# Moving one fold, one adding up and the verdict in a graph attention and convolution kernel

## The chip, the cores and the metric

The kernel runs on one core of a Trainium2 chip. The metric is the device time of the whole program in microseconds, lower is better; the kernel before takes 2567.88 us as the median of three runs.

The engines are named as in the profile: PE is TensorE, PEld its weight loads, DVE is VectorE, ACT is ScalarE, POOL is GpSimd, SP is SyncE, which here issues most DMAs.

## What is computed

For each of 32 batches of a 512 x 512 block x, with one adjacency matrix adj for all:

```
q, k, v = x @ Wq + bq, x @ Wk + bk, x @ Wv + bv         # 8 heads of 64
w   = softmax(q k^T / sqrt(64) + (-1e9 where adj == 0))  # per head, over keys
x   = layernorm(x + w v)                                 # no gain or shift
y   = adj @ x
out = layernorm(x + y @ W1 + b1)
```

All inputs and outputs are float32.

## The kernel before, in words

**Precision.** A large product is made as three passes of split factors (HIGH, REST, BOTH), each of four matmuls of 128x512. HIGH and REST gather in a "near" PSUM bank, BOTH in a "far" one. The near bank is read first, the far one is added after it: for q and k by ACT (L435) and DVE (L436), for v by DVE twice (L466, L467). There are eight banks, taken in turn.

**Order.** Everything is unrolled in a region in which each engine issues its instructions in the order in which the Python code emits them (`manual_schedule`). The order across engines comes from semaphores. `merge(units, behind)` emits unit k and then the list `behind[k]`.

**A batch.** `iteration(b)` ends batch b's attention while it projects batch b + 1. Heads come in pairs hp = 0 to 3, and pairs in groups g of two:
- `scores` makes, for each pair and each block j of keys, two score blocks on PE (L609), masks them on DVE (L611), takes exponentials on ACT (L613) and adds the blocks j on POOL into a tile `es` (L624). There are two `es` buffers; so es(b, hp) overwrites es(b, hp - 2), and es(b + 1, 0) overwrites es(b, 2).
- `fold_squares(b, hp)` turns `es` around in squares of 32 (two DVE transposes, L662) and sums them (two reductions, L664). `pass_parts` and `fetch_parts` carry the partial sums through DRAM on SP's queue (L671, L678), and `add_up` finishes the denominators of a group: a reduction and a reciprocal on DVE (L684, L685), and a sum on POOL for a guard (L686).
- `attend(b, hp)` multiplies exponentials and values on PE (L632), with `V[b, j]` for block j, j = 0 to 3 in turn. `turn_out` turns the result on DVE (L644) and sends it through DRAM; `fetch_rows` brings it back in rows (L652), `scale_rows` scales by the denominators on ACT (L698), `add_rows` adds to x on POOL (L702).

**Around the first part of the change.** For b = 0 the code emits: projections of batch 1, units 0 to 3 (q and k of blocks 0 and 1), with folds and add_up between; attend and turn_out of pairs 2 and 3; scaling of rows; then

```
        later = scores(b + 1, 0)
        run(added + later + folded[1:])
```

`scores(b + 1, 0)` emits the POOL sums of pair 0 itself and returns those of pair 1 as `later`; `added` are the residual adds of POOL. Then come units 4 to 7 of the projections, with the passing of parts behind the first, fold (1, 0) behind the third; then the values of batch 1, with `add_up(0, 1)` behind row block 0 and fold (1, 1) and DMA issues (loads of the next x in squares L232, rows L652, weight chunks L419) behind row block 1. After the values, for b = 0, come DVE turns of batch 2's x (L347), `split_last_weight` (emitted before the last three turns: ACT L766, L767, L770 and POOL L768, L771), the splits of batch 2's x (ACT L304, DVE L307, POOL L310), and iteration 1 begins with attend (1, 0) and (1, 1), their turn-outs, and scores (1, 1).

**Around the second part.** The last batch's four row blocks r end the kernel one after the other: DVE adds the far bank (L568), takes statistics (L484, L485), ACT takes the root (L488), DVE inverts it (L493) and makes a shift (L495), ACT normalises (L500), SP stores (L515). The last row block is normalised in two halves, one by DVE (L1009), one by ACT (L1011), which are stored from SP and from ACT (L1013). The guards of the whole run are summed by a 1-column matmul (L991) and compared to one number, `verdict` (L1007). After that every engine loads the verdict (L168) and branches on it (L170), past a general kernel that isn't run when the guards hold.

Of the kernel before, what the change touches and what calls it, by code (L numbers as in the profile page):

```python
# [12 lines left out]
AF = mybir.ActivationFunctionType  # L13
ALU = mybir.AluOpType
# [4 lines left out]
P = 128  # L19
# [163 lines left out]
def fast_kernel(ctx: ExitStack, tc, verdict, x, adj, Wq, bq, Wk, bk, Wv, bv, W1, b1, out):  # L183
    nc = tc.nc
# [3 lines left out]
    NB = N // P  # L188
# [11 lines left out]
    def bank(*shape):  # L200

        return psum.tile([P, *shape], FP, name="bank", tag="bank", bufs=8)
# [159 lines left out]
    def turns(b):  # L362
        return [(turn_squares, b, d) for d in range(DB)] if b < B else []

    def splits_of_x(b):
        return [[(f, b, d) for d in range(DB)] if b < B else [] for f in (high_of_x, rest_of_x, both_of_x)]
# [102 lines left out]
    def projections(b):  # L469

        return [(project, b, which, m) for which, m in SEQUENCE] if b < B else []
# [4 lines left out]
    STAT, RSTD, SHIFT, HIGHS, LOWS = {}, {}, {}, {}, {}  # L476
# [13 lines left out]
    def invert_root(t, slots):  # L490

        rstd = RSTD[t][:, slots]
        nc.vector.reciprocal(rstd, rstd)  # L493
        for slot in range(slots.start, slots.stop):
            nc.vector.tensor_scalar(SHIFT[t][:, slot:slot + 1], STAT[t][:, slot, 0:1], RSTD[t][:, slot:slot + 1], -1.0,  # L495
                                    op0=ALU.mult, op1=ALU.mult)
# [95 lines left out]
    def aggregation(b):  # L592

        return [[(f, b, d) for d in range(DB)] if b >= 0 else [] for f in (split, aggregate)]
# [31 lines left out]
    def attend(b, hp):  # L626
        po = bank(N)
        for j in range(NB):
            e = E.pop((b, hp, j))
            for s in range(2):  # L630
                h = 2 * hp + s
                nc.tensor.matmul(po[s * HD:(s + 1) * HD, :], V[b, j][:, h * HD:(h + 1) * HD], e[:, s, :],  # L632
                                 start=(j == 0), stop=(j == NB - 1))
        OUT[b, hp] = po

    def turn_out(b, hp):

        po = OUT.pop((b, hp))
        at = AT[b, hp] = work.tile([P, N], FP, name="attT")
        if b == B - 1:  # L640
            nc.scalar.activation(at, po, AF.Copy)  # L641
            return

        nc.vector.transpose(at, po)  # L644
        TURNED[b, hp] = passing.tile([P, N], FP, name="turned")
        nc.sync.dma_start(TURNED[b, hp], at)
# [26 lines left out]
    def fetch_parts(b, g):  # L673

        part = PART[b, g].rearrange("p a c h -> p a (c h)")
        passed = PASSED.pop((b, g)).rearrange("(a r) i x -> i r a x", r=SQ)
        for i in range(P // SQ):
            nc.sync.dma_start(part[i * SQ:(i + 1) * SQ, :, :], passed[i])  # L678
# [49 lines left out]
    def run(units):  # L728
        for unit in units:
            unit[0](*unit[1:])  # L730
# [3 lines left out]
    pm = bank(P)  # L734
# [46 lines left out]
    def folds(b, g):  # L781
        return [(fold_squares, b, hp) for hp in range(g * PAIRS, (g + 1) * PAIRS)]
# [5 lines left out]
    def residuals(b, g):  # L788

        return [[(f, b, hp) for hp in range(g * PAIRS, (g + 1) * PAIRS)] for f in (scale_rows, add_rows)]  # L790
# [4 lines left out]
    def merge(units, behind):  # L795

        merged = []
        for k in range(max(len(units), len(behind))):
            merged += units[k:k + 1] + (behind[k] if k < len(behind) else [])
        return merged  # L800

    def take_scores(b, g):
        run(scores(b, g))

    def iteration(b):

        units = projections(b + 1)
        scaled, added = residuals(b, 0)
        later_scaled, later_added = residuals(b, 1)
        turned, divided = turns(b + 2), splits_of_x(b + 2)  # L810
        splits, gathered = aggregation(b - 1)
        squares = [(load_squares, b + 2, d) for d in range(DB)]
        folded = folds(b, 1)

        attend(b, 0)
        turn_out(b, 0)
        sooner, later = AFTER.pop(b - 1, ([], []))
        run(sooner)
        attend(b, 1)
        turn_out(b, 1)  # L820
        if b > 0:
            fetch_parts(b, 0)
        take_scores(b, 1)
        run(later)
        waiting = [(fetch_rows, b, 0), (fetch_rows, b, 1)]
        looking = 2 <= b < 2 + NB
        look = [(look_for_low_half, b - 2)] if looking else []
        ready = 1 if looking else 0 if b < 2 else 2
        run(waiting[:ready])
        if b == 0:  # L830
            run(merge(units[:4], [waiting + [(fold_squares, b, 1), (pass_parts, b, 0), (fetch_parts, b, 0)], [],
                                  [(add_up, b, 0)],
                                  folded[:1]]))
        else:
            old, young = norm(b - 1, 1), norm(b - 1, 0)
            roots = slice(0, 2 * NB if b > 1 else NB)
            if b == 1:
                run(survey(0, 0))
            run(merge(units[:4], [waiting[ready:]
                                  + [(square_root, b - 1, roots), (add_up, b, 0), (invert_root, b - 1, roots)],  # L840
                                  folded[:1] + old[2:], [(store, b - 2)] if b > 1 else [], young[2:] + scaled]))
        attend(b, 2)
        turn_out(b, 2)
        load(b)
        if looking:
            load_adjacency_rows(b - 2)
        attend(b, 3)
        turn_out(b, 3)
        if b == 0:
            run(scaled)  # L850
        later = scores(b + 1, 0)
        run(added + later + folded[1:])

        run(merge(units[4:], [[(pass_parts, b, 1), (fetch_parts, b, 1)], look, [(fold_squares, b + 1, 0)], splits[:2]]))
        units = values(b + 1)
        chunks = [(fetch_chunk, (b + 2) * len(SEQUENCE) + n) for n in range(AHEAD)]
        squares += [(fetch_rows, b, 2), (fetch_rows, b, 3), (pass_parts, b + 1, 0)] + chunks
        run(merge(units, [[(add_up, b, 1)], [(fold_squares, b + 1, 1)] + squares, later_scaled if b == B - 2 else [],
                          turned[:1] + (later_added if b == B - 2 else [])]))
        if b == B - 2:  # L860
            load(B - 1)
        if b == 0:
            split_last_weight()
        run(merge(gathered, [[unit] for unit in turned[1:]]))
        fresh, seen, shift = survey(b, 0), survey(b - 1), biases(b - 1)
        high, rest, both = divided
        if b == 0:
            run(high + rest + both[::-1] + later_scaled + later_added)
            return
        convolve(b - 1, FIRST_TWO)  # L870
        if b == B - 2:
            run([(add_row, b - 1, 0), (add_row, b - 1, 1)] + shift[:2] + fresh + seen[:2])
            return
        run(later_scaled + later_added[:1] + [(add_row, b - 1, 0)] + shift[:1] + later_added[1:])
        run([(add_row, b - 1, 1)] + shift[1:2] + seen[:1])
        convolve(b - 1, whole(2))
        run([(add_row, b - 1, 2)] + shift[2:3] + fresh[:1])
        convolve(b - 1, whole(3))
        run(high + rest + [(add_row, b - 1, 3)] + shift[3:] + both)
        AFTER[b] = (fresh[1:] + seen[1:2], seen[2:])  # L880
# [87 lines left out]
    for b in range(B - 1):  # L968
        iteration(b)
    last_halves(B - 1)  # L970

    t = B - 1
# [17 lines left out]
    pm = bank(N)  # L990
# [4 lines left out]
    for r in range(NB):  # L995
        slot = slice(NB + r, NB + r + 1)
        add_far(t, r, FAR.pop((t, r)))
        statistics(t, 1, r)
        square_root(t + 1, slot)
        if r < NB - 1:  # L1000
            add_near(t, r + 1, NEAR.pop((t, r + 1)))
        invert_root(t + 1, slot)
        if r < NB - 1:
            normalise(t + 1, NB + r)
            store(t, [r])
        if r == NB - 2:
            nc.vector.tensor_scalar(verdict, pm[0:1, 0:1], P - 0.5, None, op0=ALU.is_lt)  # L1007
    sides = [X[t][:, NB - 1, side * D // 2:(side + 1) * D // 2] for side in range(2)]
    nc.vector.tensor_scalar(sides[0], sides[0], STAT[t + 1][:, slot.start, 0:1], RSTD[t + 1][:, slot],  # L1009
                            op0=ALU.subtract, op1=ALU.mult)  # L1010
    nc.scalar.activation(sides[1], sides[1], AF.Identity, bias=SHIFT[t + 1][:, slot], scale=RSTD[t + 1][:, slot])  # L1011
    for side, engine in enumerate((nc.sync, nc.scalar)):
        engine.dma_start(out[t, (NB - 1) * P:, side * D // 2:(side + 1) * D // 2], sides[side])  # L1013


# [22 lines left out]
```

## Time and profile before

| What | Value |
|---|---|
| runs | 2567.47, 2567.88, 2568.14 us; median 2567.88 |
| the profiled execution | 2570.15 us; its span, first to last instruction, 2568.3 us |
| granted TensorE clock | 0.999 |
| PE busy | 2558.8 us, 100% |
| DVE, ACT, POOL busy | 2058.3, 1528.5, 1751.8 us |
| one sum of POOL, L624 | 2394 to 2407 ns |
| one masking of DVE, L611 | 678 ns |
| one exponential of ACT, L613 | 1055 ns |
| one score matmul, L609; one of attend, L632; one of a pass, L424 | 598; 595; 389 to 392 ns |

Times in the profile are microseconds from the first instruction. Durations overlap on an engine: sixteen L611 take 9.62 us, 0.598 from start to start. "Idle before, releaser" names what ended an idle stretch. PE's busy time counts a matmul that is held in the array by a full bank as busy, so a stretch is also to be compared with an equal one elsewhere.

### The profile page before, as it was taken

Reading aid. Unit: us, or ns where it says so; the run is one execution under the profiler, and the core shown is the slowest. Engines: PE = TensorE matmul, PEld = TensorE weight load, DVE = VectorE, ACT = ScalarE, POOL = GpSimd, SP = SyncE. Lnnn points to the kernel's source line nnn. Section 1 sums busy time; section 2 is a strip of 40 time slices with the busy share of each in tenths; the row PEclk is TensorE's granted clock in tenths of the full one; section 3 lists DMA queues with packets and bytes.
Section 4 is the critical chain, followed back from the end, with each engine's and each line's share of the span. In section 5 each row is a group of like instructions: output and inputs, shape, how many; then the busy total and the mean of one; then the engine's idle time right before and its main releaser. Section 6 shows DMA issues by size and latency. Waiting matters only on the chain.

```text
span 2568.3 us, 36882 instructions
## 1 busy us (share of the span) xinstructions
PE 2558.8 (100%) x11324; PEld 1692.3 (66%) x11324; DVE 2058.3 (80%) x3796; ACT 1528.5 (60%) x2540; POOL 1751.8 (68%) x1104
## 2 busy tenths in 40 slices
PE   9999999999999999999999999999999999999998
PEld 6676666666676666766667676666766667666666
DVE  8878878788787887877888778877787787887878
ACT  5656655666555666556665565655657556565555
POOL 4776667666676666766767676676766766666767
PEclk9999999999999999999999999999999999999999
DMA  9655554554545645456455465554655546555441
GB/s 266 167 158 150 161 154 117 165 156 151 166 113 150 168 138 163 125 138 177 136 156 133 133 174 138 164 133 123 173 143 160 148 113 167 146 158 163 108 121 52
DMA packets 747291, 380.59 MB, mean 148 GB/s; under 512 B 594896, under 2 KB 599248, under 8 KB 747088
## 3 DMA queue, kind: packets, MB, share of 16 engines
q1 hardware_dynamic: 746656, 377.51, 53.6%
q8 instruction: 93, 1.52, 0.3%
q14 instruction: 110, 0.90, 0.1%
q10 hardware_dynamic: 432, 0.66, 0.1%
HBM read 303.57 MB, written 74.45 MB: 147 GB/s over the span
## 4 chain that ended last, share of the span: by engine, by line
PE 99%; DVE 0%; DMA 0%; ACT 0%; issue 0%; DVEq 0%
PE bank L424 55%; PE bank L609 18%; PE bank L632 17%; PE bank L533 9%; PE bank L557 0%; DMA xin<-in_x_dram 0%; DVE bnst L484 0%; DVE xlast L564 0%; DVE xlast L568 0%; PE bank L336 0%; PE bank L708 0%; DVE shift L495 0%; PE bank L738 0%; ACT attT L641 0%; ACT xlast L1011 0%
## 5 line engine op out<-in xcount | busy, mean ns | idle before, releaser
L613 ACT ACTIVATE e<-e 128x1024 f32<-128x1024 f32 x512 | 525.7, 1055 | 309.0 <-DVE e L611 269.7
L424 PE MATMUL bank<-factors,stream 128*128 128x512 f32 x3012 | 703.2, 392 | 0.0
L424 PEld LDWEIGHTS bank<-factors,stream 128*128 128x128 f32 x3012 | 560.5, 188 | 163.4 <-DVE e L611 23.5
L624 POOL TENSOR_TENSOR es<-es,e 128x1024 f32<-128x1024 f32 x256 | 616.2, 2407 | 20.1
L611 DVE SCALAR_TENSOR_TENSOR e<-gap,bank 128x512 f32<-128x512 uint8 x1024 | 617.7, 678 | 12.5 <-PE bank L609 12.5
L624 POOL TENSOR_TENSOR es<-e 128x1024 f32<-128x1024 f32 x128 | 306.4, 2394 | 425.8 <-ACT e L613 423.4
L609 PE MATMUL bank<-q,k 64*128 64x512 f32 x2048 | 462.7, 598 | 0.0
L632 PE MATMUL bank<-e,v 128*64 128x512 f32 x2048 | 453.6, 595 | 0.0
L609 PEld LDWEIGHTS bank<-q,k 64*128 64x128 f32 x2048 | 203.2, 186 | 258.0 <-issue 159.0
L424 PE MATMUL bank<-w,factors 128*128 128x512 f32 x1536 | 354.3, 389 | 0.0
L424 PE MATMUL bank<-wv,factors 128*128 128x512 f32 x1536 | 353.5, 389 | 0.0
L698 ACT ACTIVATE rows<-rows,zero,inverse 128x64 f32<-128x64 f32 x992 | 335.1, 429 | 8.5 <-DVE inverse L685 8.5
L310 POOL TENSOR_TENSOR factors<-factors,factors 128x512 fp32r<-128x512 f32 x254 | 321.3, 1290 | 25.0 <-DVE factors L307 25.0
L424 PEld LDWEIGHTS bank<-wv,factors 128*128 128x128 f32 x1536 | 288.2, 188 | 60.6 <-DVE e L611 0.8
L424 PEld LDWEIGHTS bank<-w,factors 128*128 128x128 f32 x1536 | 288.0, 188 | 60.7 <-POOL factors L310 0.4
L632 PEld LDWEIGHTS bank<-e,v 128*64 128x64 f32 x2048 | 141.4, 137 | 278.4 <-issue 264.4
L510 ACT ACTIVATE high<-xs 128x512 fp32r<-128x512 f32 x124 | 74.4, 627 | 333.5 <-PE bank L533 333.4
L511 POOL TENSOR_TENSOR low<-xs,high 128x512 fp32r<-128x512 f32 x124 | 159.3, 1296 | 155.7 <-PE bank L533 155.7
L548 POOL TENSOR_TENSOR xs<-xs,b_r 128x512 f32<-128x512 f32 x124 | 160.3, 1294 | 125.7 <-DVE xs L568 125.7
L644 DVE STREAM_TRANSPOSE attT<-bank 128x512 f32<-128x512 f32 x124 | 87.8, 708 | 155.7 <-PE bank L632 152.8
L500 ACT ACTIVATE xs<-xs,shift,rstd 128x512 f32<-128x512 f32 x248 | 181.5, 805 | 14.8 <-DVE shift L495 14.8
L702 POOL TENSOR_TENSOR xs<-xs,rows 128x512 f32<-128x512 f32 x124 | 160.7, 1307 | 22.4 <-DMA stream<-kept_q 10.2
(98 smaller groups left out, 2431.4 us busy)
## 6 DMA issues: line engine op xcount, KB each, us to landing
stream<-kept_q SPq DMA_DIRECT2D x372, 256.0 KB, 4.7
stream<-kept_k SPq DMA_DIRECT2D x372, 256.0 KB, 3.6
xin<-in_x_dram SPq DMA_DIRECT2D x496, 64.0 KB, 2.3
turned<-attT SPq DMA_DIRECT2D x124, 256.0 KB, 3.3
rows<-turned SPq DMA_DIRECT2D x496, 64.0 KB, 2.5
xs<-in_x_dram SPq DMA_DIRECT2D x31, 1024.0 KB, 5.9
out_dram<-xs SPq DMA_DIRECT2D x31, 1024.0 KB, 5.2
part<-passed SPq DMA_DIRECT2D x256, 8.0 KB, 1.7
```

Source lines behind the costliest of these rows:

```text
L310: engine.tensor_sub(both, plain(high), plain(rest))
L424: nc.tensor.matmul(pm, left(f, d), right(f, d), start=(f != REST and d == 0), stop=(f != HIGH and d == DB - 1))
L500: nc.scalar.activation(row, row, AF.Identity, bias=SHIFT[t][:, slot:slot + 1], scale=RSTD[t][:, slot:slot + 1])
L533: nc.tensor.matmul(pm, part, adjT[:, n % NB, :], start=(n == 0), stop=(n == 2 * NB - 1))
L548: nc.gpsimd.tensor_add(X[b][:, c, :], X[b][:, c, :], b1_r)
L609: nc.tensor.matmul(ps[s], keys[:, j * P:(j + 1) * P], queries, start=True, stop=True)
L611: nc.vector.scalar_tensor_tensor(e[:, s, :], gap[:, j, :], NEG * root, ps[s], op0=ALU.mult, op1=ALU.add)
L613: nc.scalar.activation(e, e, AF.Exp, scale=1.0 / root)
L624: nc.gpsimd.tensor_add(ES[b, hp], ES[b, hp] if j > 1 else E[b, hp, 0], E[b, hp, j])
L632: nc.tensor.matmul(po[s * HD:(s + 1) * HD, :], V[b, j][:, h * HD:(h + 1) * HD], e[:, s, :], start=(j == 0), stop=(j == NB - 1))
L698: nc.scalar.activation(part, part, AF.Identity, bias=zero, scale=inverse[:, c, s:s + 1])
L702: nc.gpsimd.tensor_add(cols, cols, ROWS.pop((b, hp)))
```

## The change

For b = 0 alone, `fold_squares(0, 2)` moves from behind projection unit 3 to behind the scores of batch 1's first group, ahead of `fold_squares(0, 3)`, and `add_up(0, 0)` moves from behind unit 2 to behind unit 3. At the end of the kernel the verdict's comparison moves from ahead of the last row block's far sum to behind its root; the last row block's shift is no longer made, and both its halves are normalised by DVE, which subtracts the mean and multiplies by the inverted root.

```diff
         if b == 0:
-            run(merge(units[:4], [waiting + [(fold_squares, b, 1), (pass_parts, b, 0), (fetch_parts, b, 0)], [],
-                                  [(add_up, b, 0)],
-                                  folded[:1]]))
+            run(merge(units[:4], [waiting + [(fold_squares, b, 1), (pass_parts, b, 0), (fetch_parts, b, 0)], [], [],
+                                  [(add_up, b, 0)]]))
...
         later = scores(b + 1, 0)
-        run(added + later + folded[1:])
+        run(added + later + folded[b > 0:])
...
         square_root(t + 1, slot)
         if r < NB - 1:
             add_near(t, r + 1, NEAR.pop((t, r + 1)))
-        invert_root(t + 1, slot)
-        if r < NB - 1:
+            invert_root(t + 1, slot)
             normalise(t + 1, NB + r)
             store(t, [r])
-        if r == NB - 2:
-            nc.vector.tensor_scalar(verdict, pm[0:1, 0:1], P - 0.5, None, op0=ALU.is_lt)
+    nc.vector.tensor_scalar(verdict, pm[0:1, 0:1], P - 0.5, None, op0=ALU.is_lt)
+    rstd = RSTD[t + 1][:, slot]
+    nc.vector.reciprocal(rstd, rstd)
     sides = [X[t][:, NB - 1, side * D // 2:(side + 1) * D // 2] for side in range(2)]
-    nc.vector.tensor_scalar(sides[0], sides[0], STAT[t + 1][:, slot.start, 0:1], RSTD[t + 1][:, slot],
-                            op0=ALU.subtract, op1=ALU.mult)
-    nc.scalar.activation(sides[1], sides[1], AF.Identity, bias=SHIFT[t + 1][:, slot], scale=RSTD[t + 1][:, slot])
     for side, engine in enumerate((nc.sync, nc.scalar)):
+        nc.vector.tensor_scalar(sides[side], sides[side], STAT[t + 1][:, slot.start, 0:1], rstd,
+                                op0=ALU.subtract, op1=ALU.mult)
         engine.dma_start(out[t, (NB - 1) * P:, side * D // 2:(side + 1) * D // 2], sides[side])
```

## The prediction

> **What bounds the kernel now.** I first read the page's chain of waits and the waits of TensorE (PE).
>
> ```profile
> PE 99%; DVE 0%; DMA 0%; ACT 0%; issue 0%; DVEq 0%
> ```
>
> ```profile
> PE bank L738 <- DVE attT L733: 1.1, 1, 1.1
> ```
>
> The chain is PE nearly all the way, and PE's longest recorded wait is 1.1 us, at the start. So any microsecond PE loses or wins is carried to the end; work elsewhere costs nothing until PE waits for it. Next the timelines around batch 0's first pass: PE, then VectorE (DVE), then GpSimd (POOL). Columns are start, length, engine, line, operation, tiles.
>
> ```profile
> 82.00 8.21 PE L609 MATMUL bank<-q,k 64*128 64x512 f32 x32
> 90.14 11.20 PE L424 MATMUL bank<-factors,stream 128*128 128x512 f32 x48
> 101.17 11.04 PE L424 MATMUL bank<-wv,factors 128*128 128x512 f32 x48
> 112.15 7.09 PE L632 MATMUL bank<-e,v 128*64 128x512 f32 x32
> 119.16 7.21 PE L609 MATMUL bank<-q,k 64*128 64x512 f32 x32
> 126.30 0.96 PE L424 MATMUL bank<-factors,stream 128*128 128x512 f32 x3
> ```
>
> ```profile
> 79.59 0.26 DVE L684 TENSOR_REDUCE inverse<-part 128x16 f32<-128x64 f32 x1 [6.03 <-DMA part<-passed]
> ...
> 80.60 1.29 DVE L662 STREAM_TRANSPOSE square<-es 128x512 f32<-128x512 f32 x2
> 81.82 1.24 DVE L664 TENSOR_REDUCE part<-square 128x16 f32<-128x512 f32 x2
> 82.97 1.31 DVE L644 STREAM_TRANSPOSE attT<-bank 128x512 f32<-128x512 f32 x2
> 84.20 9.62 DVE L611 SCALAR_TENSOR_TENSOR e<-gap,bank 128x512 f32<-128x512 uint8 x16
> ...
> 107.42 1.29 DVE L662 STREAM_TRANSPOSE square<-es 128x512 f32<-128x512 f32 x2
> ```
>
> Scores (1,0) take PE 82.00 to 90.14 = 8.14 us; scores (1,1) take 119.16 to 126.30 = 7.14. The 1.00 us is hidden in "busy". Its cause: the masking row L611 starts 2.20 us after PE at 82.00, but 1.16 after it at 119.16, because fold (0,2) stands in front of it. POOL:
>
> ```profile
> 87.87 2.37 POOL L624 TENSOR_TENSOR es<-e 128x1024 f32<-128x1024 f32 x1 [7.40 <-ACT e L613]
> 90.31 4.89 POOL L624 TENSOR_TENSOR es<-es,e 128x1024 f32<-128x1024 f32 x2
> 95.15 2.56 POOL L702 TENSOR_TENSOR xs<-xs,rows 128x512 f32<-128x512 f32 x2
> 97.66 2.42 POOL L624 TENSOR_TENSOR es<-e 128x1024 f32<-128x1024 f32 x1
> ```
>
> These are the sums es(1,0), the residual adds and es(1,1). There are two `es` buffers, so es(1,0) overwrites es(0,2), which the fold reads. That wait is real: the view of the tile `es` shows, for es(0,3) behind fold (0,1),
>
> ```profile
>   DVE square L662: 2.4, 1
> ```
>
> Last, the end. The branch on the verdict, L170, costs one engine much:
>
> ```profile
> L170 PEldq COMPARE_BRANCH  x1: 4069/4069/4069, 2561.7 to 2561.7; - x1
> ```
>
> **What the Trainium skill says.** "TensorE: Matmul & The Clock Gate" (section "Architectural detail: the array is 16× 32×32, not 1× 128×128"): the queues of ScalarE (ACT), VectorE and GpSimd are strict first in, first out. The trace agrees: DVE idled 6.03 us at 79.59 for add_up's DMA while k's far part, whose ScalarE half ended at 74.88, waited behind. "PSUM — Partial Sum Buffer" ("Specifications (TRN2)"): eight banks per partition. In the trace, score matmuls j restart about 0.05 us after L611 j-8 ends. "Runtime: NRT & Kernel Launch" ("Instruction fetch mechanics"): a taken branch whose target is not in the loaded pages stalls on a fetch. PE's 4.07 us agrees; the other engines' records show 0.05 to 0.07.
>
> **Part 1, removing fold (0,2) from before the scores; add_up after k's far part.** A fold is two L662 and two L664; from 80.60 to 82.97 it holds DVE 2.37 us. Without it, far k runs as soon as ACT is done, 75.0. add_up still starts at 79.59 with its DMA, and releases ACT's row scaling at 80.18 as before. Turn-out 2 runs at 80.06, turn-out 3 0.06 after attend ends, 82.13; L611 starts at PE + 1.16 = 83.16. At 82.00 a start of 2.20 gave a stall of 1.00, so the tolerance is about 1.19. **PE: -1.00 us**; scores end at 89.14, and all later PE times below are 1.00 earlier. ACT's exponentials still start at 85.54, behind its scaling (80.18 + 5.41), but catch up: ACT's last needs L611's end 92.81, so ends 93.9 instead of 94.98.
>
> **Part 2, fold (0,2) after all sixteen L611.** Queued behind it on DVE: fold (0,3), the far parts, the values. Waiting for it: POOL's es(1,0), and all of POOL behind that.
> - L611 start 83.16 + 16 x 0.598 = 92.73; the two transposes end at 94.02. POOL starts 0.14 later (as at 71.35 after 71.21): es(1,0) from **94.17 instead of 87.87**. Three adds take 7.3 to 101.5; residual adds 2.5 to 103.96; es(1,1) 7.38 to **111.34 instead of 105.04**. The emission order holds POOL's residual adds behind es(1,0).
> - DVE: fold (0,2) to 95.1, fold (0,3) to 97.5, far q2, k2, q3 to 99.3. PE's values need these banks from about 102.0 on (far pass of r = 0); free. Fold (1,0) waits for POOL until 101.57; far k3 at 103.95 to 104.6 (bank wanted at 110.2); values 0, add_up, values 1 end at 107.9. Then **fold (1,1) waits to 111.41**, and behind it L466/L467 of r = 2 end at 115.26 and of r = 3 at 116.82 (steps 2.37, 0.79, 0.77, 0.79 of the rows at 107.42 to 112.25). In the kernel before they end at 111.27 and 112.95.
> - PE's attend (1,0) would start at 111.15. Its matmuls use V[1,2] 1.77 us and V[1,3] 2.63 us after its start, 112.91 and 113.77. The old slack was 2.6 and 1.8 us. Now j = 2 starts at 115.3, ends at 116.2; j = 3 starts at 116.87. **PE: +3.10 us.**
> - What is late next: DVE's four turns L347 follow at 116.73, four L307 after them, turn-outs at 121.73 and 122.36 (5.0 us from first turn to first turn-out, as 112.86 to 117.86), L611 at 122.96. ACT is no limit: POOL's w subtractions L768 run 111.5 to 116.6, so ACT's last L770 ends at 117.2, before the first turn it needs (117.4). PE's scores (1,1) start at 119.16 - 1.00 + 3.10 = 121.26; L611 comes 1.70 after, tolerance 1.19: **+0.51 us**.
> - After that: the BOTH split of batch 2 on POOL runs 121.9 to 126.9; PE reads it after scores end at 121.26 + 7.14 + 0.51 = 128.9 and eight matmuls of 0.23, at 130.7. Exponentials start at 125.2 rather than 121.6, each 0.97, and finish with L611 again. No further stall.
> - SP's queue: pass_parts moves from 96.2 to 97.6, and the fetches, square loads and row fetches behind it by 1.4 to 2.2. The last square load is issued at some 111.9; its turn is after 116.7. Batch 2's chunks start at some 118, wanted at 128.9. Cost nothing; the cover is 10 us.
>
> Part 2 could cost below 3.6 only if POOL's chain were shorter: with the residual adds ahead of es(1,0), es(1,1) ends 2.5 us earlier and r = 3 at 114.3, a stall of 0.6. It could cost more by POOL's latency per wait. I take the working, 3.6, bounds 0.6 and 4.5.
>
> **Part 3, the tail.** Before: DVE L495 (0.21) and L1009 (0.40, started at 2563.33), ACT L1011 (2563.45, 0.60), its DMA at 2564.08, landing 2.6 later. After: the verdict (0.13) no longer holds back L568: -0.07. The shift operation L495 is gone: the first half starts at 2563.13. The second follows by 0.13 to 0.40 (start offset of L495 to L1009; length of L1009); I take 0.32, end 2563.85, DMA 2563.88: **-0.20**. The verdict fits in DVE's 0.36 us wait for the square root, but is written at 2562.62 instead of 2561.09. PE's load and branch wait for it: PE's event, at 2565.85 before, comes 1.52 later, 2567.37 if the 4.07 us fetch repeats. In the trace's records SP's last but one wait before its drain, at 2567.36, is on that semaphore. Then SP's drain ends at 2567.63 instead of 2567.55: **+0.1 in all** instead of -0.20. Bounds: -0.2 (shorter fetch) to +0.5 (longer).
>
> **Sum:** -1.00 + 3.10 + 0.51 + 0.1 = +2.7 us. The profiled execution took 2570.15 with a span of 2568.3; its span becomes 2571.0. The median of the runs shown, 2567.88, is 2.27 below it; the same sum gives **2570.6**.
>
> **Rivals.**
> - *A, no new PE stall (14%)*: V[1,3] is in time, by the residual adds going first or fold (0,2) going earlier. For it: the 1.00 us stall is certain to go, and POOL idles 7.40 us before es(1,0). Against it: in the emission order es(1,0) precedes them. -1.00 - 0.2: 2566.7.
> - *B, slower by over 0.2% (6%)*: the delay reaches batch 2. POOL runs es(1,1), eight w subtractions and the four BOTH splits in one chain; from PE's 130.7 on, each microsecond they are later is paid again. My margin is 3.8 us; a chain 6.8 later than worked out gives +2.7 + 3.0 = 2573.6. Against it: POOL has idle time in every iteration to catch up, 10.24 us before 150.62.
> - *C, the stall is there but small (10%)*: bound 0.6, no second stall: -1.00 + 0.6 + 0.1, 2567.6 to 2569.5.
> - The forecast (70%): 2569.7 to 2571.6, from 0.3 to 0.5 us for each waiting step.
>
> **Numbers.** Outside a range of 2567.6 to 2571.9 stay A and B, 20%. A measurement of this kernel can tell about 0.2%, 5.1 us, from no change: below 2562.7 nothing above reaches (2%), above 2573.0 only B (6%); within, 92%.
>
> **What would show it.** Scores (1,0) 7.14 us long; POOL's es(1,0) near 94.2 waiting for L662; DVE idle some 3.5 us before the fold at 111.4; a gap inside PE's L632 near 113; PE's branch ending near 2567.3. Wrong, if POOL starts es(1,0) before 92, or the residual adds precede it, or PE runs unbroken through L632.

## The result, and the profile after

| | us |
|---|---|
| before, median of 12 runs | 2567.84 (2567.47 to 2568.81) |
| changed, median of 12 runs | 2574.34 (2573.44 to 2574.53) |
| ratio, with its 95% interval | 1.0024 (1.0017 to 1.0032) |
| profiled execution of the changed kernel, and its span | 2574.53, 2572.7 |

The changed kernel is 6.5 us slower; 2.7 slower was forecast, with a range that ended at 2571.9. The two spans, 2568.3 and 2572.7, differ by 4.4 only. Matched matmul by matmul, the profile of before runs ahead by 4.83 us at 126.3 us and by 2.99 us at 2560, falling evenly on the way: that one execution was 0.08% longer throughout, which is most of what its 2570.15 us lie above the median of 2567.84. So stretches are compared below, not distances from the start.

PE's timeline of the changed kernel, in the window shown of before:

```profile
82.35 7.28 PE L609 MATMUL bank<-q,k 64*128 64x512 f32 x32
89.56 11.18 PE L424 MATMUL bank<-factors,stream 128*128 128x512 f32 x48
100.58 11.04 PE L424 MATMUL bank<-wv,factors 128*128 128x512 f32 x48
111.55 1.94 PE L632 MATMUL bank<-e,v 128*64 128x512 f32 x8
115.73 7.04 PE L632 MATMUL bank<-e,v 128*64 128x512 f32 x24 [2.25 <-DVE v L467]
122.70 8.50 PE L609 MATMUL bank<-q,k 64*128 64x512 f32 x32
131.13 9.18 PE L424 MATMUL bank<-factors,stream 128*128 128x512 f32 x39
```

Scores (1,0) now take 89.56 - 82.35 = 7.21 us: PE no longer waits there. But attend (1,0), at 111.55, breaks off after eight matmuls for a value of VectorE (2.25 us), and scores (1,1) take 8.43 instead of 7.14. From the start of attend to the end of those scores PE needs 131.13 - 111.55 = **19.58 us; it was 126.30 - 112.15 = 14.15**. That stretch, 14.15 undisturbed, is the yardstick for the experiments. VectorE and then GpSimd, same kernel:

```profile
79.24 0.27 DVE L684 TENSOR_REDUCE inverse<-part 128x16 f32<-128x64 f32 x1 [3.04 <-DMA part<-passed]
...
83.58 9.66 DVE L611 SCALAR_TENSOR_TENSOR e<-gap,bank 128x512 f32<-128x512 uint8 x16 [0.40 <-PE bank L609]
93.16 1.30 DVE L662 STREAM_TRANSPOSE square<-es 128x512 f32<-128x512 f32 x2
...
111.82 1.31 DVE L662 STREAM_TRANSPOSE square<-es 128x512 f32<-128x512 f32 x2 [3.56 <-POOL es L624]
...
114.99 0.69 DVE L467 TENSOR_TENSOR v<-bank,v 128x512 f32<-128x512 f32 x1
...
116.38 0.69 DVE L467 TENSOR_TENSOR v<-bank,v 128x512 f32<-128x512 f32 x1
116.99 2.48 DVE L347 STREAM_TRANSPOSE turn<-xin 128x512 f32<-128x512 f32 x4
119.39 4.65 DVE L307 SCALAR_TENSOR_TENSOR factors<-factors,turn 128x512 fp32r<-128x512 f32 x4
123.97 1.30 DVE L644 STREAM_TRANSPOSE attT<-bank 128x512 f32<-128x512 f32 x2
125.20 9.61 DVE L611 SCALAR_TENSOR_TENSOR e<-gap,bank 128x512 f32<-128x512 uint8 x16
```

```profile
94.60 2.41 POOL L624 TENSOR_TENSOR es<-e 128x1024 f32<-128x1024 f32 x1 [14.47 <-DVE square L662]
97.09 4.88 POOL L624 TENSOR_TENSOR es<-es,e 128x1024 f32<-128x1024 f32 x2
101.92 2.57 POOL L702 TENSOR_TENSOR xs<-xs,rows 128x512 f32<-128x512 f32 x2
104.45 2.40 POOL L624 TENSOR_TENSOR es<-e 128x1024 f32<-128x1024 f32 x1
106.93 4.86 POOL L624 TENSOR_TENSOR es<-es,e 128x1024 f32<-128x1024 f32 x2
...
116.87 5.42 POOL L771 TENSOR_TENSOR w<-w,xs 128x512 fp32r<-128x512 f32 x4
```

Read across: the fold at 93.16 frees es(0,2), and GpSimd starts es(1,0) only at 94.60, after 14.47 us of idling, and ends es(1,1) near 111.8. VectorE waits 3.56 us for that, so V[1,2], the value that PE waits for, is written at 115.68 (114.99 + 0.69), and PE goes on at 115.73. The last value, V[1,3], follows at 117.07. A second thing is new: four L307 take 4.65 us. They now run beside L771 of GpSimd. In the kernel before they took 2.67 us, and L771 was all but over when they began:

```profile
115.27 2.67 DVE L307 SCALAR_TENSOR_TENSOR factors<-factors,turn 128x512 fp32r<-128x512 f32 x4
```

```profile
110.55 5.03 POOL L771 TENSOR_TENSOR w<-w,xs 128x512 fp32r<-128x512 f32 x4
```

The end, the changed kernel's branch of PE and its last two stores (columns: issues, KB, microseconds to landing):

```profile
L170 PEldq COMPARE_BRANCH  x1: 4409/4409/4409, 2566.5 to 2566.5; - x1
```

```profile
out_dram<-xlast SPq DMA_DIRECT2D x1, 128.0 KB, 4.2
out_dram<-xlast ACTq DMA_DIRECT2D x1, 128.0 KB, 4.3
```

The same two stores in the kernel before:

```profile
out_dram<-xlast SPq DMA_DIRECT2D x1, 128.0 KB, 2.4
out_dram<-xlast ACTq DMA_DIRECT2D x1, 128.0 KB, 2.6
```

From the start of PE's last pass (its last L424) to the end of the span it is 9.42 us now, 7.95 before. Five more profiles of kernels with the tail of before have 7.89 to 8.16.

### The profile page after: what moved, and what is told of

Its sections match the earlier page's. It is cut to its first block, busy times and chain, and to the rows that moved or that the text cites. A ratio compares the mean times of both kernels' runs of the same rounds, so it can differ in the third digit from the quotient of the medians.

```text
span 2572.7 us, 36885 instructions
## 1 busy us (share of the span) xinstructions
PE 2559.9 (99%) x11324; PEld 1694.4 (66%) x11324; DVE 2060.0 (80%) x3796; ACT 1527.8 (59%) x2539; POOL 1750.1 (68%) x1104
## 3 DMA queue, kind: packets, MB, share of 16 engines
q8 instruction: 93, 1.52, 0.2%
## 4 chain that ended last, share of the span: by engine, by line
PE 98%; DVE 1%; POOL 1%; issue 0%; ACT 0%; POOLq 0%; DVEq 0%
PE bank L424 54%; PE bank L609 18%; PE bank L632 17%; PE bank L533 9%; POOL es L624 0%; DVE e L611 0%; PE bank L557 0%; PE bank L738 0%; DVE bnst L484 0%; DVE xlast L564 0%; PE bank L336 0%; POOL xs L702 0%; DVE square L662 0%; DVE xlast L568 0%; PE bank L708 0%
## 5 line engine op out<-in xcount | busy, mean ns | idle before, releaser
L424 PE MATMUL bank<-factors,stream 128*128 128x512 f32 x3012 | 701.1, 392 | 0.0
L424 PEld LDWEIGHTS bank<-factors,stream 128*128 128x128 f32 x3012 | 560.6, 188 | 161.2 <-DVE e L611 23.5
L611 DVE SCALAR_TENSOR_TENSOR e<-gap,bank 128x512 f32<-128x512 uint8 x1024 | 617.9, 681 | 12.5 <-PE bank L609 12.5
L632 PE MATMUL bank<-e,v 128*64 128x512 f32 x2048 | 455.5, 597 | 2.2 <-DVE v L467 2.2
L424 PE MATMUL bank<-w,factors 128*128 128x512 f32 x1536 | 354.3, 389 | 0.0
L424 PE MATMUL bank<-wv,factors 128*128 128x512 f32 x1536 | 353.5, 389 | 0.0
L310 POOL TENSOR_TENSOR factors<-factors,factors 128x512 fp32r<-128x512 f32 x254 | 320.8, 1285 | 24.8 <-DVE factors L307 24.4
L424 PEld LDWEIGHTS bank<-wv,factors 128*128 128x128 f32 x1536 | 288.3, 188 | 60.5 <-DVE e L611 0.8
L424 PEld LDWEIGHTS bank<-w,factors 128*128 128x128 f32 x1536 | 288.1, 188 | 60.6 <-POOL factors L310 0.4
L632 PEld LDWEIGHTS bank<-e,v 128*64 128x64 f32 x2048 | 141.6, 137 | 282.3 <-issue 264.7
```

The source lines that it names most:

```text
L310: engine.tensor_sub(both, plain(high), plain(rest))
L424: nc.tensor.matmul(pm, left(f, d), right(f, d), start=(f != REST and d == 0), stop=(f != HIGH and d == DB - 1))
L611: nc.vector.scalar_tensor_tensor(e[:, s, :], gap[:, j, :], NEG * root, ps[s], op0=ALU.mult, op1=ALU.add)
```

## The experiments

Each is compared with the kernel before, run on the same chip. It took 2567.85 us beside the folds alone, the early fold, both halves on VectorE and the verdict behind the root; 2569.85 us, 0.08% more, on the chip of the third buffer, L771, the residual adds and the last experiment; and 2567.99 us beside the other three. Medians are of 13 to 21 runs. The numbers in brackets are the ratio to the kernel before and its 95% interval.

**The folds alone.** The diff of the change without its tail.

> The two moves in batch 0 (fold (0,2) behind the scores, add_up behind k's far part), with the tail as in the kernel before. Theory: the folds cost PE some 4.5 us net (scores (1,0) -0.9, attend (1,0) and (1,1) +4.1, scores (1,1) +1.3), the tail the remaining 1.5 to 2 us: 4.3 to 5.0 us slower than before. Rival, that the folds cost what was forecast (2.6) and the tail 3.9: 2.6 us slower. Rival, that the whole 6.5 are the folds' and the tail is free: 6.5.

2573.30, **+5.45** (1.0020, 1.0012 to 1.0028), more than the 4.3 to 5.0 of the theory. By the medians the folds hold 5.45 of the 6.5 us and the tail about 1.04. The first rival, 2.6 us, lies outside the interval, which is 3.1 to 7.2 us. The second, 6.5, lies inside; against it speaks that the single times hardly touch: 2573.47 us at most here, 2573.44 at least for the whole change. The timeline of PE in this kernel:

```profile
115.79 1.08 PE L632 MATMUL bank<-e,v 128*64 128x512 f32 x4 [2.23 <-DVE v L467]
117.18 4.51 PE L632 MATMUL bank<-e,v 128*64 128x512 f32 x20 [0.31 <-DVE v L467]
121.62 2.85 PE L609 MATMUL bank<-q,k 64*128 64x512 f32 x12
124.82 6.48 PE L609 MATMUL bank<-q,k 64*128 64x512 f32 x20 [0.35 <-DVE attT L644]
131.23 4.16 PE L424 MATMUL bank<-factors,stream 128*128 128x512 f32 x17
```

The stretch is 131.23 - 111.62 = 19.61, the same as in the changed kernel, though its inside differs: attend ends at 121.62 instead of 122.70, and scores (1,1) wait the longer for it. Attend takes 10.00 us, 2.99 more than undisturbed (119.16 - 112.15 = 7.01), the scores 9.61, 2.47 more. What ends the stretch is VectorE's L611, not attend.

**A third buffer.** `bufs=PAIRS + 1` for `es`, with the biases left out to make room; the output lacks them.

> The kernel of the first experiment (both moves in batch 0, tail as before), with three es buffers instead of two, so that es(1,0) needn't wait for fold (0,2). To make room, the biases bv and b1 are left out: a row of the adjacency is added in the place of each, and their two loads are gone. Theory, that GpSimd's wait for fold (0,2) is the whole cost: es(1,0) starts with the exponentials near 87.9, fold (1,1) waits for nothing, PE has no gap in attend (1,0): 5.5 us faster than the first experiment, 0.3 to 0.9 faster than before (2567.0 to 2567.6). Rival, that VectorE's two folds in a row (2.37 us more in one place) delay the values by themselves: 2 us or more slower than before.

2569.82, **-0.03** (1.0001, 0.9993 to 1.0009): the whole 5.45 us is gone, though the 0.3 to 0.9 that was expected on top is not seen. GpSimd, then PE:

```profile
87.23 2.38 POOL L624 TENSOR_TENSOR es<-e 128x1024 f32<-128x1024 f32 x1 [7.61 <-ACT e L613]
```

```profile
111.48 7.09 PE L632 MATMUL bank<-e,v 128*64 128x512 f32 x32
118.50 7.21 PE L609 MATMUL bank<-q,k 64*128 64x512 f32 x32
125.63 7.59 PE L424 MATMUL bank<-factors,stream 128*128 128x512 f32 x32
```

The stretch is 14.15 again, with the same instructions as in the kernel of the first experiment but for L466, which reads a row of the adjacency. So two folds in a row on VectorE, which this kernel still has, cost nothing there, and the rival falls; the wait for the buffer, with what followed from it, was all. The four L307 took 2.67 us here.

**The L771 subtractions moved** out of L307's way, behind the sums of scores (1,1); `finish_last_weight` makes them there:

```diff
         for d in range(DB):
             nc.scalar.activation(w[:, d, :], plain(w1[:, HIGH, d, :]), AF.Copy, scale=EPSILON)
-            nc.gpsimd.tensor_sub(w1[:, BOTH, d, :], plain(w1[:, REST, d, :]), w[:, d, :])
...
         run(later)
+        if b == 1:
+            finish_last_weight()
```

> The kernel of the first experiment, with GpSimd's last four subtractions of the split of W1 (L771) moved behind the sums of scores (1,1), away from VectorE's split of x (L307). Theory, that L307 and L771 lock each other out (both read two operands in SBUF): L307 takes 2.7 us for four instead of 4.7, the masking of scores (1,1) starts up to 2 us earlier: 1.3 to 2.0 us faster than the first experiment, 2571.3 to 2572.0; attend (1,0) keeps its gap. Rival, that L307 is slow since it waits for ScalarE's L304: 2573.3 as before the move.

2573.61, **+3.76** (1.0014, 1.0007 to 1.0020), 1.7 less than the folds alone. The two intervals overlap; the profile is clearer. VectorE:

```profile
119.61 2.46 DVE L307 SCALAR_TENSOR_TENSOR factors<-factors,turn 128x512 fp32r<-128x512 f32 x4
121.98 1.31 DVE L644 STREAM_TRANSPOSE attT<-bank 128x512 f32<-128x512 f32 x2
```

The same four L307 take 2.46 us, the stretch 129.16 - 111.77 = 17.39, 2.22 less than with the folds alone, and PE's gap of 2.25 us in attend stays. ScalarE's L304 took 2.35 us in both kernels, so the rival falls. That the two engines exclude each other in SBUF is what the Trainium skill states ("SBUF — State Buffer", section "SBUF: two separate sides": a VectorE operation with two SBUF inputs and a GpSimd operation that reads SBUF take one port pair by turns); the runs show the effect, 2.2 us on four instructions, not the port.

**Residual adds first.** `run(added)` ahead of `scores(1, 0)` for b = 0.

> The kernel of the first experiment, with the two residual adds of batch 0 emitted ahead of the scores, so that GpSimd runs them while it waits for fold (0,2). Theory: es(1,1) ends 2.5 us earlier, near 109.3, V[1,3] is ready near 114.5, PE's gap in attend (1,0) shrinks to 0.3 or less, but L307 still meets L771 until 119.4, so the masking of scores (1,1) starts near 122.8 and PE stalls there: 2.5 us faster than the first experiment, 2570.8. Rival, the bound of the prediction (0.6 us in attend, nothing after): 2568.2.

2572.34, **+2.49** (1.0010, 1.0004 to 1.0017): 3.0 less than the folds alone, where 2.5 was worked out; the stretch, 128.28 - 111.23 = 17.05, is 2.56 shorter. The gap in attend shrank to 0.28, L307 still took 4.62 us beside L771, and L611 began at 122.34 (122.8 expected). The rival, nothing lost after attend, falls.

**Fold (0,2) early**, in the time in which VectorE waits for add_up's transfer:

```diff
-                                  [(add_up, b, 0)],
-                                  folded[:1]]))
+                                  [], folded[:1] + [(add_up, b, 0)]]))
```

> The kernel before with fold (0,2) and add_up both behind k's far part, the fold first, so that the fold lies in the 3 us in which VectorE waits for add_up's transfer; the tail as before. Theory: scores (1,0) lose their 0.9 to 1.0 us of waiting, GpSimd's es(1,0) starts with the exponentials at about 87.9 as before, nothing waits later: -0.9 us. Rival, that what hurts is any earlier start of the scores: +2 or more.

2567.54, **-0.31** (0.9999, 0.9990 to 1.0007), which can't be told from no change; -0.9 was expected. Scores (1,0) took 7.14 in its profile, so the wait did go. But it was smaller than believed. The next experiment kept the folds of before, and PE's scores (1,0) there took 89.53 - 82.19 = 7.34, not 8.14:

```profile
82.19 7.42 PE L609 MATMUL bank<-q,k 64*128 64x512 f32 x32
89.53 11.17 PE L424 MATMUL bank<-factors,stream 128*128 128x512 f32 x48
```

```profile
78.99 0.26 DVE L684 TENSOR_REDUCE inverse<-part 128x16 f32<-128x64 f32 x1 [5.22 <-DMA part<-passed]
```

There the transfer landed 0.6 us earlier (78.99 against 79.59), so fold (0,2) ended earlier too and 0.8 us of the wait was gone. In the other four profiles with the folds of before (the verdict at three places, the whole tail alone) they took 7.38 to 7.55. The wait that the change removes depends on when a DMA lands.

**Both halves on VectorE**, the verdict early:

> The kernel before with one thing changed: both halves of the last row block on VectorE and no shift for it; the verdict early as before. Theory: the stores are issued 0.13 to 0.2 us earlier and land after 2.4 to 2.6 as before: -0.15 us, hardly to be told from no change. Rival, that two stores 0.33 us apart from VectorE make the landing late: +1.5.

2567.90, **+0.05** (1.0000, 0.9992 to 1.0009): no change that can be told; the stores landed after 2.6 us. In its profile the way from PE's last pass to the end is 7.81 us, 0.14 less than in that of before, as worked out, and below the 7.89 to 8.16 of the others with the tail of before. The early landing rules the rival out.

**The verdict later**, at three places, else the kernel before.

```diff
         statistics(t, 1, r)
...
-        if r == NB - 2:
-            nc.vector.tensor_scalar(verdict, pm[0:1, 0:1], P - 0.5, None, op0=ALU.is_lt)
```

In the first it stands behind the last row's root, in the second ahead of its `statistics`, in the third behind VectorE's half.

> The kernel before with one thing changed: the verdict's comparison stands behind the last row block's root, as in the changed kernel; its halves as before. Theory: PE's branch, and with it its fetch of 16384 bytes, starts about 1.5 us later and shares a DMA engine with the last stores, which then land 4.2 us after their issue instead of 2.4 to 2.6: +1.5 to +1.8 us. Rival, that only PE's branch counts and sets the end: +0.1 to +0.3. Rival, that the two halves on VectorE make the late landing: -0.07, no change.

> The kernel before with the verdict's comparison between the last row block's far sum and its statistics, about 0.65 us later than before and 0.9 earlier than behind the root. Theory, that what costs is PE's fetch of 16384 bytes meeting the last stores on a DMA engine: the fetch ends before the stores' packets, so little or nothing: 0.0 to +0.3 us. Rival, that every delay of the verdict is paid in full by PE's branch: +0.65.

> The kernel before with the verdict's comparison behind VectorE's half of the last row block, about 2.5 us later than before. Theory: PE's event comes some 4.8 us after the verdict and now sets the end by itself: +1.3 to +1.9 us. Rival, that only the meeting of fetch and stores costs: no more than the +1.1 of the verdict behind the root, perhaps less, since the fetch then starts behind most packets of the stores.

| verdict | median, difference | stores land after | PE's branch takes | last pass to end |
|---|---|---|---|---|
| ahead of the statistics | 2567.74, -0.25 | 2.2 and 2.6 | 3.81 | 7.84 |
| behind the root | 2568.91, +1.06 | 4.3 and 4.3 | 4.66 | 9.55 |
| behind VectorE's half | 2568.81, +0.82 | 1.7 and 1.8 | 4.43 | 9.50 |

The intervals of the ratios, 0.9991 to 1.0008, 0.9995 to 1.0012 and 0.9995 to 1.0012, each hold 1, so the medians carry little by themselves; the profiles say what happens. The last stores' landing, first of the verdict behind the root, then behind the half:

```profile
out_dram<-xlast SPq DMA_DIRECT2D x1, 128.0 KB, 4.3
out_dram<-xlast ACTq DMA_DIRECT2D x1, 128.0 KB, 4.3
```

```profile
out_dram<-xlast SPq DMA_DIRECT2D x1, 128.0 KB, 1.7
out_dram<-xlast ACTq DMA_DIRECT2D x1, 128.0 KB, 1.8
```

Packets in the changed kernel's records (start, length, queue, bytes) tell why:

```
2567.584  1.934  q8 instruction  16384
2569.515  0.141  q1 out_dram      1024    (seven more of 1024 follow, to 2570.29)
2570.292  0.046  q10 out_dram     1024    (seven more, to 2570.63)
```

An instruction fetch of 16384 bytes holds up sixteen rows of the last stores: their packets begin as it ends, at 2569.52, while all other rows had gone by 2569.1. (The fetch is taken to be PE's: in both kernels it starts 1.06 us after PE's branch.) With the verdict behind the root alone it ended at 2564.62, and the sixteen rows began there at 2564.62 too. In the profile of before the like fetch ran from 2562.78 to 2564.29, ahead of those rows. With the verdict behind VectorE's half the stores are out in time, but PE's event comes at 2566.78, 3.0 us after the second store's landing was seen at 2563.75, and sets the end by itself. So the profiles show what the theories described. The sizes by the medians are smaller: +1.06 behind the root where 1.5 to 1.8 was expected, +0.82 behind the half for 1.3 to 1.9. Ahead of the statistics the rival's +0.65 lies inside the interval too; against it speak only the landing in time and the 7.84 us.

One thing more stands in the changed kernel's records: PE's event comes at 2571.00, some 0.2 us ahead of the last store, which is seen at 2571.18; in the kernel before it was 0.87 us ahead (2565.85 and 2566.72). Where PE's event came last (the verdict behind VectorE's half), the span ended 0.98 us after it. By that, as an estimate, PE's event alone would have ended the changed kernel at 2571.97 and not at 2572.74: of the 1.47 us that the way to the end grew, some 0.7 go with PE's event and 0.8 with the stores.

**The whole tail alone.**

> The whole second part of the change alone (verdict behind the root, both halves on VectorE), folds and add_up as before. Theory: the difference of the changed kernel and the first experiment, +1.0 us. Rival, that the parts add differently: the +1.06 of the late verdict less the 0.15 of the halves, +0.9, or more than 1.5, as in the one profile of the changed kernel.

2569.06, **+1.07** (1.0003, 0.9995 to 1.0012), stores landing after 4.0 us, 9.20 us from the last pass to the end. The interval holds 1, so the median alone does not show the cost of the tail; the 9.20, 9.42 and 9.55 us of the three profiles with the verdict behind the root, against 7.72 to 8.16 in the eight with the verdict as before, do. The sum of both parts, 5.45 + 1.07, is the 6.5 of the change.

**Fold early and both halves on VectorE**, for a version that beats both.

> Fold (0,2) and add_up behind k's far part, the fold first, and both halves of the last row block on VectorE with the verdict early. Theory: the sum of the two alone, -0.3 and 0.0 to -0.15: 2567.4. Rival, no gain: 2567.85.

2569.33, **-0.52** (0.9998, 0.9989 to 1.0006). It is faster than the changed kernel; that it is faster than the kernel before isn't shown.

## Why the prediction was wrong, step by step

- **What bounds the kernel; the buffer wait.** Right. The row that was to show it came as described: es(1,0) at 94.60 (94.17 forecast), after a wait of 14.47 us for L662; the wait of VectorE 3.56 us (3.5); PE's gap in L632 where it was put. The third buffer shows that this wait is the cause.
- **"PE: -1.00 us" for part 1.** Mechanism right, size off. It came from one execution in which the transfer landed late. With unchanged folds the same scores took 7.34 to 7.55 in five other profiles, so 0.2 to 0.4 us were there to win. The changed kernel's scores took 7.21; with the fold early, -0.31 was measured.
- **"+3.10" and "+0.51" for attend and scores (1,1).** 3.61 was forecast, 5.43 measured (19.58 - 14.15). The folds alone show which of the two was wrong: attend lost 2.99, near the 3.10, but scores (1,1) lost 2.47. The step that failed is "5.0 us from first turn to first turn-out, as 112.86 to 117.86": it took 123.97 - 116.99 = 6.98. The four L307 were priced at 2.67 us from a row that had run almost free of GpSimd. The working itself had moved GpSimd's chain by 6 us, so that L771 fell beside them; it checked whether that chain was late for ScalarE, and not what VectorE would share with it. Moving L771 took the stretch to 3.24 over the undisturbed one, near the 3.61.
- **"+0.1 in all" for the tail.** +1.04 to +1.07. The gain of 0.20 was right in kind (0.14 in the profile of the halves alone, nothing to be told in the medians). That the late verdict delays PE's fetch was foreseen; but it was priced as PE's own event only, 1.52 us later, with the load and the branch as long as before and the stores landing as before. PE's load took 0.77 and its branch 4.41 us (0.49 and 4.07 before), so that its event came 2.15 us later, counted from the last pass; and the fetch met the stores, which landed 1.7 to 1.8 us later.
- **Where it shows up in the sum.** -1.00, +3.61, +0.1 became about -0.3, +5.4 and +1.0. These add up to 6.1; the missing 0.4 us are not explained; single runs of the kernel before differ by up to 1.34 us. All three errors had the same sign. The second and the third took a duration from the old place of an operation to a place with another neighbour; the first took it from a single execution.
- **Rivals.** A (no new stall) needed the residual adds first, and even then 2.49 was lost; with the fold early, its other way, no new stall came (-0.31). The result lies where only B was expected, but B's way (a late BOTH split of batch 2) did not happen: L310 ended at 129.15 and PE ran on. C's "small stall" is nearest to the run with the residual adds first, which lost more than C allowed.

## What to carry to other kernels

When a step that reads a buffer is moved back, the next writer of that buffer moves back with it, and everything in order behind that writer; it is priced at the engine that finally waits, with the new neighbours of every operation on the way. An operation that is slow only beside a certain other one is cheap or dear by accident of time, so a shift by some microseconds needs the durations of both cases. At the end of a program a branch is work too: its fetch moves with the value it waits for, and can meet the last stores.

## What the runs showed of the hardware that was not expected

After the gap of 2.25 us PE's granted clock was halved for 3.4 us in the changed kernel's profile (columns: stretch, length, busy times, then the granted clock, DMA):

```profile
113.50:115.70 2.20, 0.00 (x0) 0.00 (x0) 2.10 (x5) 1.02 (x2) 2.20 (x3) 1.00 0.61 96
115.73:119.17 3.44, 3.44 (x8) 0.96 (x10) 3.33 (x6) 2.63 (x5) 3.44 (x3) 0.50 0.65 96
119.17:122.70 3.53, 3.53 (x18) 0.98 (x14) 3.53 (x3) 3.53 (x11) 3.12 (x3) 1.00 1.00 338
```

Eight matmuls took twice their time, some 1.7 us. The folds alone had a gap of 2.23 us and kept the full clock:

```profile
115.70:119.17 3.47, 3.07 (x14) 0.97 (x16) 3.37 (x7) 2.59 (x5) 3.47 (x4) 1.00 0.65 107
```

In both kernels attend and scores (1,1) end 19.6 us after attend began, since VectorE's L611, at 125.20 and 125.29, decides: the halved clock cost nothing here.

Why only one of two equal gaps halved the clock can be worked out from the clock's records in the traces. The halved stretch lasted 3.413 us, and every stretch of full clock, in all thirteen profiles, is a whole multiple of that: 32 and 717 times in the changed kernel, 749 to 751 times in the others. Cut into pieces of this length from the start of the first such stretch, the changed kernel has PE busy for 34% of the piece that ends at 115.72, where the clock fell. With the folds alone the gap lies across two pieces, busy 68% and 58%; with L771 moved they are busy 65% and 60%, and the clock stayed full. At the ends of the programs it is the same: the clock fell behind the first piece that was busy 44% or less, and behind none that was busy 50% or more. So, as far as these profiles go, it matters how the gap lies to these pieces, and not only how long it is. No run moved the gap alone.
